# Weight sums of five product sets: made beside their use from quadrants loaded twice, instead of stored to and loaded from DRAM

## The chip, the core and the metric

The kernel runs on one core of a Trainium2 chip, all in float32. The metric is the device time of one execution in microseconds (us). TensorE multiplies, VectorE (DVE), ScalarE (ACT) and GpSimd (POOL) do elementwise work, and SyncE (SP) issues nearly all DMAs, in program order: a DMA whose data is not ready holds back every DMA behind it.

## What is computed

With x of 2048 rows by 512 columns (2 x 1024 x 512, flattened):

```python
xn = layernorm(x)
w_masked = weight * (block_sums(mask) > 0)      # 512 x 512, blocks of 32 x 32
s = xn @ w_masked.T
nx = xn * rsqrt(mean(xn**2) + 1e-5) * ln_w
g, u = nx @ gate_w.T, nx @ up_w.T               # 1792 wide each
ffn = (silu(g) * u) @ down_w.T
out = x + s * silu(ffn)
```

What matters here is `ln_w`, by which the columns of `gate_w` and `up_w` are scaled, and the mask on `weight`.

## The kernel before

**The algorithm.** Each matrix product is made by a seven-product scheme (of Strassen's kind, in Winograd's form) at two levels. At the outer level both matrices are cut in four quadrants. Seven "sets", numbered in the order 1, 2, 6, 5, 7, 3, 4, each multiply one weight block by one block of x. Sets 1 and 2 use weight quadrants as they are; sets 6, 5, 7, 3 and 4 use sums of quadrants (4 is a quadrant itself). Within a set the same scheme runs again with seven products of a 128 x 128 weight block by a 128 x 512 block of x, numbered 1, 5, 2, 6, 3, 7, 4 in their order in time.

**The groups.** The gate and up weights make seven groups (`G = 7`, g = 0 to 6), and the masked weight is an eighth (g = 7, `g == G` in the code). A group has four weight quadrants `(R, K)`, each 128 partitions by 512 columns (256 KB). `K` is the half of the columns that `ln_w` scales. Outer sums for one group are 7 = (0,0) - (1,0), 5 = (1,0) + (1,1), 6 = block 5 - (0,0) and 3 = (0,1) - block 6.

**The order of the work.** It is written out by hand. `at(pos, fn)` puts a call at a position; all calls are sorted by position and issued in that order (last lines of the kernel function). One position is one product of 512 columns, two matmul instructions. An *instance* is one set of one group, and starts every 7 positions. Part one runs sets 1 and 2 of all eight groups (instances 0 to 15, positions 0 to 111). Part two runs sets 6, 5, 7, 3, 4 of group 0, then of group 1 and so on (instances 16 to 55, positions 112 to 391). So a group in part two takes 35 positions; `rest` is the position of its first product. A third part multiplies by `down_w` in the same way (position 392 = `END` on).

**Inside an instance** (`instance`): at offsets 0, 2, 3, 4, 6, 8, 12 the products are made into PSUM banks X, Y and Z. Product 7 of an instance is added into the bank that product 6 has just filled, so a *snap*, a DVE add at offset 5 that reads the bank first, must be done by offset 8. A *seed*, an ACT copy at offset 1, fills bank Z before offset 3. The kernel divides PSUM into 8 banks of 512 columns: 3 of X, 2 of Y, 1 of Z and 2 of V; gates (`silu`) and a few others take turns in V.

**The weights before.** In part one, each group's four quadrants are loaded (`load_a`), scaled in SBUF on ACT (`scale_a`, two instructions of 256 columns per quadrant; for g = 7 `mask_a` on POOL), and POOL makes the four outer sums (`outer_a`, 128 x 512 each, at p + 1 where p is the position of the group's set 1; p + 15 for g = 7). `store_w` writes the five blocks (1280 KB) to `w_dram`. For part two `load_w` brings them back 29 positions ahead of the group (11 for g = 0). Four POOL instructions of 128 x 640 (`inner_a`, from rest - 13, or rest - 9 for g = 0) then make the inner sums of all five sets at once.

**What else the steps touch.** `summed` adds two finished results of a set on POOL or DVE, and `done` then makes silu(gate) x up for the set's rows: ACT's gate, DVE's multiplication (`h_out`, line 404), and `h_sum`, eight POOL subtractions per group, each stored to `h_dram` by SP. `outer_d(f)` makes the outer sums of the down weights of group f: four DVE operations of 128 x 256 at offsets 30 to 36 of the group's part two, and a store at 37. Almost every add stands under line 98, the helper `add`. The last set of the third part makes its last four products in two column halves (`last_four`), so that the end of the kernel (silu, multiply, add, store: `finish`) works on 256 columns.

Of the kernel before, what the change touches and what calls it, by code (L numbers as in the profile page):

```python
# [31 lines left out]
def tile_masked_linear_gated_ffn(  # L32
# [23 lines left out]
    dw_dram = tc.dram_tile([4, P, G, 256], F32, name="dw_dram")  # L56
    w_dram = tc.dram_tile([G + 1, P, 5, W], F32, name="w_dram")

# [30 lines left out]
    def slots(i, n):  # L89
        return mem[:, i : i + n, :]  # L90
# [3 lines left out]
    def bank(tag, name):  # L94
        return ps.tile([P, W], F32, tag=tag, name=name, bufs=PSB[tag])

    def add(eng, o, a, b, op=ALU.add):
        eng.tensor_tensor(o, a, b, op)  # L98
# [144 lines left out]
    BLOCKS = (6, 5, 7, 3, 4)  # L243
    aq, aop, ablk, wblk = {}, {}, {}, {}

    def q_slot(g):
        return F["v5"] + 4 if g % 2 else F["q"]

    def w_slots(g):

        if g == 0:
            return F["q"], F["a1"] + 4
        return (F["s"], F["s"] + 5) if g % 2 else (F["q"], F["a1"] + 4)

    def load_a(g, R, K):
        i = q_slot(g) + (1, 4)[K] if R else F["a1"] + 2 * (g % 3) + K
        aq[g, R, K] = mem[:, i, :]
        nc.sync.dma_start(aq[g, R, K], gu[g, R, K] if g < G else wm[R, K])

    def scale_a(g, R, K, eng=act):  # L260
        for c in range(2):
            v = aq[g, R, K][:, c * 256 : (c + 1) * 256]
            if eng is pool:
                nc.gpsimd.tensor_scalar(v, v, lnw_sb[:, 2 * K + c : 2 * K + c + 1], None, ALU.mult)
                continue
            nc.scalar.mul(v, v, lnw_sb[:, 2 * K + c : 2 * K + c + 1])

# [15 lines left out]

    def mask_a(R, K):
        v = aq[G, R, K].rearrange("p (b j) -> p b j", j=BLK)
        k = keep[:, 2 * R + K, :].unsqueeze(2).to_broadcast([P, 16, BLK])
        nc.gpsimd.tensor_tensor(v, v, k, ALU.mult)

    def outer_a(g, q, eng):

        o = ablk[g, q] = mem[:, q_slot(g) + BLOCKS.index(q), :]
        a, b, op = {
            7: lambda: (aq[g, 0, 0], aq[g, 1, 0], ALU.subtract),
            5: lambda: (aq[g, 1, 0], aq[g, 1, 1], ALU.add),
            6: lambda: (ablk[g, 5], aq[g, 0, 0], ALU.subtract),
            3: lambda: (aq[g, 0, 1], ablk[g, 6], ALU.subtract),
        }[q]()
        add(eng, o, a, b, op)

    def store_w(g):  # L300
        nc.sync.dma_start(w_dram[g], slots(q_slot(g), 5))

    def load_w(g):
        i, _ = w_slots(g)
        nc.sync.dma_start(slots(i, 5), w_dram[g])

# [81 lines left out]
    def group(g, where):  # L388
# [39 lines left out]
        def summed(dst, src, into, then=None, engines=(pool,) * 4):  # L428

            def after(i, pos):  # L430
                at(pos + 1.2, lambda: add(engines[i], into(i), dst(i), src(i)))
                if then:
                    then(i, pos + 3.2)
            return after
# [6 lines left out]
            5: (None, v5, summed(v5, acc, vc)),  # L441
            7: (acc, acc, summed(v5, acc, v5, done(1, 1, v5), (dve, dve, pool, pool))),
            3: (vc, vc, done(0, 1, vc)),
# [42 lines left out]
    def outer_d(f):  # L486

        a = slots(F["a1"] + 2, 2).rearrange("p s w -> p (s w)").rearrange("p (b w) -> p b w", w=256)
        o = mem[:, F["v5"] + 8, :].rearrange("p (b w) -> p b w", w=256)
        (a11, a12, a21, a22), (s3, s1) = (a[:, b] for b in range(4)), (o[:, b] for b in range(2))  # L490

        def load():
            for b in range(4):
                nc.sync.dma_start(a[:, b], down[b // 2, b % 2, :, f])

        def store():
            nc.sync.dma_start(dw_dram[0:2, :, f].rearrange("b p w -> p b w"), a[:, 0:2])
            nc.sync.dma_start(dw_dram[2:4, :, f].rearrange("b p w -> p b w"), o)

        return [load, lambda: add(dve, s3, a11, a21, ALU.subtract), lambda: add(dve, s1, a21, a22),  # L500
                lambda: add(dve, a11, s1, a11, ALU.subtract), lambda: add(dve, a12, a12, a11, ALU.subtract), store]

# [49 lines left out]
    def down_instance(o, q, where_, prior, dest, after):  # L552
# [7 lines left out]

        last_set, halves = q == DOWN[-1], (slice(0, W // 2), slice(W // 2, W))

        def last_four(products):

            four = [(lambda k=k: ds[q][4][:, k, :], lambda k=k: dt[q, 4][:, k, :]) for k in range(K3)]
            four.append((lambda: dq[q][:, G - 1, P :], lambda: dh[q][:, 0, G - 1, :]))
            for half in halves:
                for w, b in four:
                    def one(w=w, b=b, half=half):
                        nc.tensor.matmul(st[half.start][:, half], w(), b()[:, half], start=False, stop=True,  # L570
                                         skip_group_check=True)
                    products.append(one)

        def base_of_last():
            for half in halves:
                st[half.start] = bank("X", f"half_{half.start}")
                add(dve, st[half.start][:, half], st["x"][:, half], prior(2)[:, half])

        products = []
        for m, key in ((1, "x"), (5, "y"), (6, "x"), (2, "z"), (None, "z"), (None, "v"), (7, "x"), (3, "y"), (None, "y"),  # L580
# [9 lines left out]
            for k in range(K3):  # L590
                b = {1: lambda k=k: dh[q][:, 0, k, :], 2: lambda k=k: dh[q][:, 0, K3 + k, :],
                     3: lambda k=k: dh[q][:, 1, K3 + k, :]}.get(m, lambda k=k, m=m: dt[q, m][:, k, :])
                products.append((key, lambda k=k, m=m: ds[q][m][:, k, :], b, k == 0 and m in (1, 5)))
        assert len(products) == (29 if last_set else 25)
        for k, p in enumerate(products):
            if callable(p):
                at(where_(21) + (k - 21) / 2, p)
            else:
                at(where_(k), mm, k, *p)
# [29 lines left out]
        if last_set:  # L629
            at(where_(17) + 0.1, base_of_last)  # L630
            for half, pos in zip(halves, (where_(23), where_(25))):
                finish(1, 0, 2, yacc(2), pos, dve, half, lambda half=half: st[half.start][:, half])

# [14 lines left out]
    for K in range(2):  # L648
        at(T(-10), load_a, 0, 0, K)
    at(T(-10), load_x, 1)  # L650
    for R, K, g in ((0, 0, 1), (0, 1, 1), (1, 0, 0), (1, 1, 0)):
        at(T(-10), load_a, g, R, K)
    at(T(-10), load_x, 2)
    for R, K, g in ((0, 0, 2), (0, 1, 2), (1, 0, 1), (1, 1, 1)):
        at(T(-10), load_a, g, R, K)
    at(T(-10), load_x, 3)
# [13 lines left out]
    for i in range(TT):  # L670
# [5 lines left out]
        for c in range(KC):  # L676
            at(T((10.2, 10.6, 11.0, 11.8)[c] + 0.1 * i), transpose, 0, c, (2, 3, 0, 1)[i], "XYYX"[c])
            at(T(15.3 + 0.4 * c + 0.1 * i), transpose, 1, c, (2, 3, 0, 1)[i], "XVVY"[c])
    at(T(6.0), scale_a, 0, 0, 0, pool)
    at(T(8.2), scale_a, 0, 0, 1, pool)  # L680
    for c in range(KC):
# [5 lines left out]
    for q in (1, 2):  # L687
        for k in (0, 1):
            for n in (0, 1):
                at(8, outer_b, q, k, n, None)  # L690
    at(T(16.4), scale_a, 1, 0, 0)
    for pos, (R, K, g) in zip((5.2, 8.7, 9.8), ((0, 1, 1), (1, 0, 0), (1, 1, 0))):
        at(pos, scale_a, g, R, K)
    for i in range(TT):
# [26 lines left out]


    for g in range(G + 1):
        p, rest = 7 * where[g, 1], 7 * where[g, BLOCKS[0]]
        prepare = scale_a if g < G else lambda g, R, K: mask_a(R, K)
        for K in range(2):
            if g > 2:
                at(p - 22, load_a, g, 0, K)
            if g > 1:
                at(p - (10.4, 7.3)[K], prepare, g, 0, K)  # L730
                at(p - 10, load_a, g, 1, K)
            if g > 0:
                at(p - ((3.1, 1.9) if g != 2 else (4.3, 3.1))[K], prepare, g, 1, K)
        if g:
            plan(p - 7, 1, inner_a(g, 1))
        else:
            plan(T(7.4), 0, inner_a(0, 1, 0, 1))
            plan(T(10.0), 0, inner_a(0, 1, 1, 1))
        sums = {0: 10, G: p + 15}.get(g, p + 1)
        for i, q in enumerate((7, 5, 6, 3)):  # L740
            at(sums + 1.6 * i, outer_a, g, q, pool)
        at(sums + 7.5, store_w, g)
        at(rest - 29 if g else rest - 11, load_w, g)
        plan(rest - 13 if g else rest - 9, 2.5, inner_a(g, 2, 0, 5))
    for f in range(G):
        for off, fn in zip((8, 30, 32, 34, 36, 37), outer_d(f)):
            at(7 * where[f, BLOCKS[0]] + off, fn)
# [24 lines left out]
    for o, q in enumerate(DOWN):  # L772
        if o == 0:
            todo = [(p, 7 * where[4, 6] + 4 * k) for k, p in enumerate((b11, b12, b22, b21, e0, e1))]
        elif o == 1:
            todo = [(p, END - 22 + 7 * p[0]) for p in (b11, b21, e0, b12, b22, e1)]
        else:
            d = D(o - 2)
            todo = [(b11, d(4)), (b12, d(4) + 0.1), (b21, d(14)), (b22, d(21)), (e0, d(25) + 1), (e1, d(25) + 1.1)]
        for part, pos in todo:  # L780
            at(pos, load_h, q, (H0, H1)[o % 2], part)
# [94 lines left out]
```

## Time and profile before

| | |
|---|---|
| median of 3 runs (lowest, highest) | 524.22 us (522.89, 524.28) |
| the profiled execution's own time | 523.43 us |
| its span, first to last instruction | 521.6 us |
| granted TensorE clock | 0.999 |
| busy: PE, DVE, ACT, POOL | 508.3, 384.6, 153.4, 376.1 us |
| DMA | 138.35 MB, mean 265 GB/s |

The profiled execution's own time is 1.83 us more than its span. Times inside the trace are from the span's start. Part one runs to about 119.6 us, part two to about 365 us. In a timeline line the columns are start, length from the first start to the last end, engine, source line, operation, output<-input, shapes and a count; a bracket holds the idle time of the engine just before and what ended it. Matmuls of 512 columns start every 0.43 us when nothing holds them, though each is shown 0.59 us long, because they overlap: a pair is shown as 1.02 and takes 0.86, two pairs are shown as 1.88 and take 1.72. So a shown idle time of PE is some 0.16 us shorter than the time lost, which is best read from the distance between starts.

### The profile page before, as it was taken

What the parts mean: (1) busy time and instruction counts of PE and PEld (TensorE: products, weight loads), DVE (VectorE), ACT (ScalarE), POOL (GpSimd) and SP (SyncE); (2) the same over time, 40 slices, a digit from 0 to 9 for tenths busy, and PEclk for the clock granted to TensorE, in tenths of its full rate; (3) what the DMA queues carried; (4) which work ended last, traced back from release to release, by engine and by line L of the source; (5) the groups of instructions that cost most, each with busy time, mean ns of one, the idle gap of its engine ahead of it and who ended that gap; (6) DMA issues with size and microseconds to landing.
All of it is one profiled execution on the core that took longest, in us unless ns stands there. A gap on an engine that the chain in (4) does not pass through costs nothing.

```text
span 521.6 us, 4847 instructions
## 1 busy us (share of the span) xinstructions
PE 508.3 (97%) x1269; PEld 230.2 (44%) x1269; DVE 384.6 (74%) x557; ACT 153.4 (29%) x286; POOL 376.1 (72%) x301
## 2 busy tenths in 40 slices
PE   8999999989999999999999999998999999999996
PEld 8444543433444444444444444443444444444443
DVE  6898789846796968869696886989645655456735
ACT  3859764431232332223233222320101101001111
POOL 5596569987996978869688886967553564739960
PEclk9999999999999999999999999999999999999999
DMA  8579979779738485675988666599897599476472
GB/s 306 219 273 340 360 238 352 291 269 385 273 139 286 182 300 203 233 261 167 403 326 268 256 239 235 197 343 357 301 386 259 187 350 354 157 251 196 156 232 80
DMA packets 60314, 138.35 MB, mean 265 GB/s; under 512 B 5744, under 2 KB 13184, under 8 KB 56192
## 3 DMA queue, kind: packets, MB, share of 16 engines
q1 hardware_dynamic: 60000, 137.53, 73.4%
q10 hardware_dynamic: 288, 0.52, 0.3%
q8 instruction: 10, 0.16, 0.1%
q14 instruction: 16, 0.13, 0.1%
HBM read 81.40 MB, written 56.63 MB: 265 GB/s over the span
## 4 chain that ended last, share of the span: by engine, by line
PE 73%; DVE 11%; DMA 7%; POOL 4%; issue 3%; ACT 1%; SPq 0%; DVEq 0%; POOLq 0%
PE x L338 24%; PE dx L559 14%; PE y L338 13%; PE dy L559 8%; DVE mem L98 7%; PE z L338 6%; PE dz L559 5%; POOL mem L98 3%; DMA w_dram<-mem 2%; DVE mem L404 2%; DMA mem<-w_dram 2%; DMA mem<-h_dram 1%; PE dv L559 1%; DMA mem<-in_mask 1%; PE pt L156 1%
## 5 line engine op out<-in xcount | busy, mean ns | idle before, releaser
L98 POOL TENSOR_TENSOR mem<-mem 128x512 f32<-128x512 f32 (+4 forms) x266 | 343.3, 1311 | 108.8 <-ACT mem L363 24.5
L338 PE MATMUL x<-mem 128*128 128x512 f32 x448 | 214.5, 595 | 2.8 <-DVE mem L98 2.4
L338 PEld LDWEIGHTS x<-mem 128*128 128x128 f32 x448 | 83.3, 190 | 110.9 <-issue 90.4
L98 DVE TENSOR_TENSOR mem<-x,mem 128x512 f32<-128x512 f32 x136 | 92.3, 684 | 42.8 <-PE x L338 41.6
L338 PE MATMUL y<-mem 128*128 128x512 f32 x224 | 114.7, 594 | 3.1 <-POOL mem L98 1.9
L98 DVE TENSOR_TENSOR mem<-mem 128x512 f32<-128x512 f32 (+2 forms) x93 | 108.6, 1171 | 8.2 <-PE dx L559 4.4
L559 PE MATMUL dx<-mem 128*128 128x512 f32 x174 | 78.3, 592 | 0.0
L98 DVE TENSOR_TENSOR mem<-y,mem 128x512 f32<-128x512 f32 x96 | 65.7, 684 | 15.0 <-PE y L338 11.4
L338 PEld LDWEIGHTS y<-mem 128*128 128x128 f32 x224 | 41.9, 190 | 55.9 <-issue 45.6
L345 ACT COPY z<-x 128x512 f32<-128x512 f32 x55 | 31.4, 571 | 119.5 <-PE x L338 117.9
L338 PE MATMUL z<-mem 128*128 128x512 f32 x112 | 57.4, 594 | 0.8 <-ACT z L345 0.8
L559 PEld LDWEIGHTS dx<-mem 128*128 128x128 f32 x174 | 33.1, 190 | 41.6 <-issue 40.9
L559 PE MATMUL dy<-mem 128*128 128x512 f32 x98 | 44.5, 592 | 0.0
L399 ACT ACTIVATE gate<-mem 128x512 f32<-128x512 f32 x56 | 33.2, 603 | 21.5 <-DVE mem L98 11.2
L404 DVE TENSOR_TENSOR mem<-gate,mem 128x512 f32<-128x512 f32 x56 | 37.3, 678 | 0.5 <-ACT gate L399 0.3
L532 POOL TENSOR_TENSOR mem<-mem 128x512 f32<-128x512 f32 x16 | 24.4, 1526 | 17.7 <-DMA mem<-s_dram 17.4
L338 PEld LDWEIGHTS z<-mem 128*128 128x128 f32 x112 | 21.0, 190 | 27.3 <-issue 22.7
L98 DVE TENSOR_TENSOR mem<-z,mem 128x512 f32<-128x512 f32 x41 | 28.0, 682 | 4.6 <-PE z L338 3.2
L559 PEld LDWEIGHTS dy<-mem 128*128 128x128 f32 x98 | 18.6, 190 | 23.4 <-issue 23.0
L542 ACT ACTIVATE silu<-mem 128x512 f32<-128x512 f32 x15 | 9.0, 602 | 64.6 <-DVE mem L98 48.3
L98 DVE TENSOR_TENSOR mem<-dx,mem 128x512 f32<-128x512 f32 x16 | 11.1, 691 | 20.0 <-PE dx L559 20.0
L559 PE MATMUL dz<-mem 128*128 128x512 f32 x56 | 25.2, 592 | 0.0
(61 smaller groups left out, 222.9 us busy)
## 6 DMA issues: line engine op xcount, KB each, us to landing
h_dram<-mem SPq DMA_DIRECT2D x98, 256.0 KB, 2.6
mem<-h_dram SPq DMA_DIRECT2D x28, 768.0 KB, 6.5
w_dram<-mem SPq DMA_DIRECT2D x8, 1280.0 KB, 6.1
mem<-w_dram SPq DMA_DIRECT2D x8, 1280.0 KB, 8.2
acc_dram<-mem SPq DMA_DIRECT2D x8, 1024.0 KB, 6.3
mem<-acc_dram SPq DMA_DIRECT2D x8, 1024.0 KB, 4.8
mem<-in_gu SPq DMA_DIRECT2D x28, 256.0 KB, 5.0
s_dram<-mem SPq DMA_DIRECT2D x16, 256.0 KB, 4.5
```

What stands on the lines that cost most here:

```text
L98: eng.tensor_tensor(o, a, b, op)
L156: nc.tensor.transpose(pt[t, c][:, i * P : (i + 1) * P], xt[t, i][:, c * P : (c + 1) * P], ident)
L338: nc.tensor.matmul(st[key], weights(g, q, m), operand(q, m), start=first and not (key == "z" and seeded), stop=True, skip_group_check=True)
L345: nc.scalar.copy(st["z"], st["x"])
L399: nc.scalar.activation(gate[key], t(), AF.Silu)
L404: nc.vector.tensor_mul(a(), gate[key], b())
L532: at_later.append(lambda: nc.gpsimd.tensor_tensor(s_tile, s_tile, rms_bc[t], ALU.mult))
L542: nc.scalar.activation(b[0][:, part], y[:, part] if source is None else source(), AF.Silu)
L559: nc.tensor.matmul(st[key], w(), b(), start=first and key != "z", stop=True, skip_group_check=True)
```

## The change

- `store_w`, `load_w`, `w_dram` and the sums of part one are gone. Part one loads, scales and uses only the two quadrants with R = 0.
- In part two, `load_block` loads all four quadrants of a group 29 positions ahead, by four DMAs of 256 KB. `outer_a` returns nine steps, at rest - 19.9 to rest - 13.95: ACT makes two scaled blocks in SBUF (four instructions of 256 columns) and three scaled copies in banks of V (six instructions of 256 columns), and DVE makes four sums of 512 columns that each read one such bank. Group 7 has its four quadrants masked on POOL at rest - 20.5, and ACT's copies are plain ones of 512 columns.
- `inner_a` of part two starts at rest - 13 for every group.
- `outer_d`: ACT copies two blocks into a V bank, three DVE sums read the bank, the fourth sum goes to POOL; offsets 24.6 to 27.5, and the store at 30.
- Set 7 of group 7 makes all four `summed` adds on POOL; two of them were on DVE.
- The last four products are made in three column parts of 256, 128 and 128.

```diff
-    def store_w(g):
-        nc.sync.dma_start(w_dram[g], slots(q_slot(g), 5))
-    def load_w(g):
-        nc.sync.dma_start(slots(i, 5), w_dram[g])
+    def scaled(o, a, g, K, eng=act):
+        if g == G:
+            if o is not a:
+                nc.scalar.copy(o, a)
+            return
+        for c in range(2):
+            cols, w = slice(c * 256, (c + 1) * 256), lnw_sb[:, 2 * K + c : 2 * K + c + 1]
+            if eng is pool:
+                nc.gpsimd.tensor_scalar(o[:, cols], a[:, cols], w, None, ALU.mult)
+            else:
+                nc.scalar.mul(o[:, cols], a[:, cols], w)
+    def load_block(g):
+        i, _ = w_slots(g)
+        wblk[g] = [mem[:, i + k, :] for k in range(5)]
+        for k, (R, K) in ((1, (1, 0)), (4, (1, 1)), (0, (0, 0)), (3, (0, 1))):
+            nc.sync.dma_start(wblk[g][k], gu[g, R, K] if g < G else wm[R, K])
+    def outer_a(g):
+        b = wblk[g]
+        v = {}
+        def in_bank(k, K):
+            v[k] = bank("V", f"a{k}_{g}")
+            scaled(v[k], b[k], g, K)
+        return [lambda: scaled(b[2], b[1], g, 0), lambda: scaled(b[4], b[4], g, 1), lambda: in_bank(1, 0),
+                lambda: in_bank(0, 0), lambda: add(dve, b[1], v[1], b[4]),
+                lambda: add(dve, b[2], v[0], b[2], ALU.subtract), lambda: add(dve, b[0], b[1], v[0], ALU.subtract),
+                lambda: in_bank(3, 1), lambda: add(dve, b[3], v[3], b[0], ALU.subtract)]
...
-            7: (acc, acc, summed(v5, acc, v5, done(1, 1, v5), (dve, dve, pool, pool))),
+            7: (acc, acc, summed(v5, acc, v5, done(1, 1, v5), (dve, dve, pool, pool) if g < G else (pool,) * 4)),
...
-        return [load, lambda: add(dve, s3, a11, a21, ALU.subtract), lambda: add(dve, s1, a21, a22),
-                lambda: add(dve, a11, s1, a11, ALU.subtract), lambda: add(dve, a12, a12, a11, ALU.subtract), store]
+            v[0] = bank("V", f"down_{f}").rearrange("p (b w) -> p b w", w=256)
+            nc.scalar.copy(v[0], a[:, 0::2])
+        return [load, in_bank, lambda: add(dve, s3, v[0][:, 0], a21, ALU.subtract), lambda: add(dve, s1, v[0][:, 1], a22),
+                lambda: add(dve, a11, s1, v[0][:, 0], ALU.subtract), lambda: add(pool, a12, a12, a11, ALU.subtract), store]
...
-        last_set, halves = q == DOWN[-1], (slice(0, W // 2), slice(W // 2, W))
+        last_set, parts = q == DOWN[-1], (slice(0, W // 2), slice(W // 2, 3 * W // 4), slice(3 * W // 4, W))
...
-        sums = {0: 10, G: p + 15}.get(g, p + 1)
-        for i, q in enumerate((7, 5, 6, 3)):
-            at(sums + 1.6 * i, outer_a, g, q, pool)
-        at(sums + 7.5, store_w, g)
-        at(rest - 29 if g else rest - 11, load_w, g)
-        plan(rest - 13 if g else rest - 9, 2.5, inner_a(g, 2, 0, 5))
+        at(rest - 29, load_block, g)
...
+        at(rest - 20, block_sums)
+        if g == G:
+            for k, (R, K) in ((1, (1, 0)), (4, (1, 1)), (0, (0, 0)), (3, (0, 1))):
+                at(rest - 20.5, lambda k=k, R=R, K=K: mask_a(wblk[G][k], R, K))
+        for k, off in enumerate((-19.9, -19.3, -18.1, -17, -15.95, -15.94, -15.93, -15.3, -13.95)):
+            at(rest + off, lambda g=g, k=k: todo[g, k]())
+        plan(rest - 13, 2.5, inner_a(g, 2, 0, 5))
     for f in range(G):
-        for off, fn in zip((8, 30, 32, 34, 36, 37), outer_d(f)):
+        for off, fn in zip((8, 24.6, 26.05, 26.06, 26.07, 27.5, 30), outer_d(f)):
             at(7 * where[f, BLOCKS[0]] + off, fn)
```

## The prediction, made before the changed kernel had run

> **What bounds the kernel.** I read the busy times by stage first, then what PE waits for, then the places of those waits in the timeline. Columns of the stages: stretch, its length, busy time (and count) of PE, PE's weight loads, DVE, ACT, POOL, then clock and DMA.
>
> ```profile
> 15.00:120.00 105.00, 100.34 (x265) 45.02 (x266) 85.09 (x142) 63.63 (x130) 78.13 (x74) 1.00 0.79 293
> 151.00:334.00 183.00, 181.69 (x421) 79.14 (x419) 147.22 (x229) 51.38 (x91) 148.56 (x110) 1.00 0.72 254
> 334.00:366.00 32.00, 30.49 (x70) 13.24 (x71) 29.79 (x38) 6.14 (x11) 22.98 (x16) 1.00 0.89 323
> 366.00:514.00 148.00, 148.00 (x346) 65.54 (x345) 84.42 (x85) 17.02 (x29) 87.17 (x60) 1.00 0.71 251
> ```
>
> PE is the bound nearly everywhere. The change leaves its products as they are, so only PE's holes, the start and the tail can move. The waits of PE (total us, times, longest) name who makes the holes:
>
> ```profile
> PE x L338 <- DVE mem L98: 2.4, 9, 0.4
> PE y L338 <- POOL mem L98: 1.9, 1, 1.9
> PE y L338 <- DVE mem L98: 1.2, 1, 1.2
> PE z L338 <- ACT z L345: 0.8, 2, 0.5
> PE pm L281 <- DVE mem L404: 0.6, 1, 0.6
> PE x L338 <- DMA mem<-w_dram: 0.3, 1, 0.3
> ```
>
> Three kinds of place, from the timelines of PE, DVE, POOL and ACT:
>
> ```profile
> 104.98 1.88 PE L338 MATMUL x<-mem 128*128 128x512 f32 x4
> 108.73 1.12 PE L338 MATMUL y<-mem 128*128 128x512 f32 x2 [1.86 <-POOL mem L98]
> ...
> 241.68 1.02 PE L338 MATMUL x<-mem 128*128 128x512 f32 x2
> 242.93 1.13 PE L338 MATMUL x<-mem 128*128 128x512 f32 x2 [0.23 <-DVE mem L98]
> ...
> 361.33 1.88 PE L338 MATMUL x<-mem 128*128 128x512 f32 x4
> 364.37 1.13 PE L338 MATMUL y<-mem 128*128 128x512 f32 x2 [1.16 <-DVE mem L98]
> ```
>
> At 108.73 two pairs should have taken 1.72; the distance is 3.75, so 2.03 are lost, and 0.10 more because the pair after a stall takes 0.96 (1.12 shown) and not 0.86. In this way I get all holes after 30 us:
>
> - Part one: 0.56 (40.20, snap late on DVE), 0.53 (42.45, seed late on ACT), 0.37 (80.7, DVE), 0.73 (85.80, DVE), 2.13 (108.73, POOL), and 0.77 at 119.61 and 123.24 (the load from `w_dram`, then POOL's 640-wide sums behind it). Sum 5.09.
> - At the group borders of part two, a hole of 0.49 at 154.77, 181.86, 212.39, 242.93, 303.50 and 334.02. Sum 2.94.
> - Before the third part 0.60 (352.64) and 1.42 (364.37). Sum 2.02.
>
> **Part one.** Removed from POOL: 32 outer sums at 1.27 each, 41 us, of which ten lie in this one stretch:
>
> ```profile
> 81.48 21.80 POOL L98 TENSOR_TENSOR mem<-mem 128x512 f32<-128x512 f32 x17
> ```
>
> POOL ran without a gap up to the late inner sum at 107.95 that PE waits for. Ten sums and two maskings less there are 14.8 us; the hole of 2.13 goes, and nothing else is near: DVE sat idle 4.1 us before 112.47. The 0.77 goes too: group 0's quadrants are now loaded some 25 us ahead (29 positions of 0.8585), and POOL's inner sums move from 119.70 into an idle time that it had there (4.3 us, waiting for `w_dram`) and into what is freed. 42.45: ACT did the R = 1 scalings (0.41 apart) and waited 0.59 for one of group 2's or 3's quadrants just before the table load and the gates that delayed the seed. With 28 ACT instructions less in part one it is early: 0.53 goes. 40.20: DVE worked without a gap from 28.2 to 40 and three tiny operations took 0.64, 0.52 and 1.02 where the same ones elsewhere take 0.31, 0.16 and 0.16; POOL's outer sums ran all that time. They are gone, DVE gains some 1.5, and 0.56 goes. 80.7 and 85.80: here DVE was held in an add of 1.74 beside POOL's sums of x, which stay. I take half of 1.10. Part one: 2.13 + 0.77 + 0.53 + 0.56 + 0.55 = **-4.5**; bounds -5.1 and -2.9 (only the first two).
>
> **The group border in part two.** Before, DVE is held by one SBUF sum of `outer_d` and the snap comes late:
>
> ```profile
> 239.05 1.28 DVE L404 TENSOR_TENSOR mem<-gate,mem 128x512 f32<-128x512 f32 x2
> 240.25 1.43 DVE L98 TENSOR_TENSOR mem<-mem 128x256 f32<-128x256 f32 x1
> 241.60 0.68 DVE L98 TENSOR_TENSOR mem<-z,mem 128x512 f32<-128x512 f32 x1
> 242.20 0.68 DVE L98 TENSOR_TENSOR mem<-x,mem 128x512 f32<-128x512 f32 x1
> ```
>
> The same sum takes 0.41 when POOL does not run beside it, and DVE operations that read a PSUM bank take 0.68 whether it runs or not. So this 1.43 is gone. What is late next? I followed both queues by hand through this group (its first product at 241.68).
>
> DVE: a queued add takes 0.60. The snap at 228.14 is followed by three of the new sums (to 230.55), set 7's first `summed` add, a total, the fourth new sum (231.75 to 232.35) and the second `summed` add. The total that was made at 231.65 starts at 233.1 and ends at 233.8; the product that needs it is due at 241.68 - 9 x 0.8585 = 233.95. Just in time. ACT's copies are no limit: loads issued near 219.7, 5.0 to landing (median of `in_gu`), seed to 225.3, four scalings of 0.41 to 227.0, and bank copies of 0.37 to 0.50 per 256 columns (a silu of 256 columns between banks, a scaling within SBUF; no row has this pairing): the second copy is there by 228.5, needed at 229.35.
>
> POOL: its first 640-wide sum now reads the fourth new sum and starts at 232.45, not 230.90. From there to the end of set 7's third `summed` add it needed 238.66 - 230.90 = 7.76; now a 256-wide down sum (0.73) stands before that add, and 0.18 of a collision with DVE goes. It ends at 240.75. DVE's second gate multiplication reads it, and that stood at 239.65: DVE waits, and behind it in the queue are z's total and the snap, which ends at 242.63. PE wants it at 242.54 (242.93 before). **So the new wait takes the place of most of the old one**: 0.24 instead of 0.49, six times: **-1.5**. Bounds: 0 (-2.9), and 0.25 worse each (+1.5), since every 0.1 that POOL starts later is 0.1 for PE.
>
> [...]
>
> **Before the third part.** DVE sheds two adds (0.88 and 1.04) between 352.5 and 355, but POOL's `h_sum`s, 0.75 later by the above, hold SP's load of the first down quadrant (issued at 340.58, 6.3 to landing), for which POOL waited 4.29 at 346.92 and, behind it, DVE and PE at 352.64. From there PE, not DVE, sets the times until the last 1536-wide adds. I take **+0.5**; bounds -1.4 (two adds less) and +1.2.
>
> **Tail.** The last columns go through silu, multiply and add at 128 instead of 256 columns (0.37, 0.42, 0.42), but DVE has two operations more in a queue that is full from 516.2. **-0.2**; bounds -0.4 and +0.8 (16 matmuls of 128 columns at 0.11 like the transposes, or at the 0.19 of a weight load). DMA moves 16 x 1280 KB less and 16 x 256 KB more, 16.8 of 138 MB; in the stage where it was fullest no wait of PE is on a transfer that this makes shorter, so I count 0.
>
> **Sum.** -4.5 - 1.5 + 0.5 - 0.2 = -5.7. Against the profiled execution's 523.43 this is **517.7 us**. The three runs' median is 0.8 above that execution, the lowest 0.5 below.
>
> **Rivals.**
> 1. *The border stays.* POOL's late start eats all of the group's gain, or up to 0.25 more each. For: the snap misses by 0.1 as it is. Against: POOL has 5.8 idle of 30.5 per group. Time: 523.43 - 4.5 + 0.5 - 0.2 = 519.2, up to 520.7.
> 2. *All holes of part two go* (POOL starts early enough), and all of part one's: 523.43 - 5.1 - 2.9 - 1.0 = 514.4.
> 3. *A loop of transfers and sums bounds the group: slower.* SP issues the loads behind the sixth `h_sum` store of the group before. From that sum's end: 0.45 to issue, 5.0 landing, ACT to the second bank copy 3.15, DVE's queue to the fourth sum 3.1, POOL from the first 640-wide sum to the next sixth `h_sum` 17.9 (230.90 to 249.05 before, less 0.74 idle and 0.25 of collisions, plus the 0.73): 29.6, against 35 x 0.8585 = 30.05 for PE. It decides from 0.45 us more. At the 6.9 of `in_down` in place of 5.0 it is 31.5, 1.45 per group, six groups: 523.43 - 4.5 + 8.7 = 527.6. For: before, this loop was some 3 us shorter, as POOL read the loaded blocks directly. Against: fewer bytes are under way, and 5.0 was measured in the fuller part one.
> 4. *It does nothing*: part one's waits reappear on DVE, the border stays: 522 to 525.
>
> **Numbers.** Chances: forecast 0.48, rival 1 0.16, rival 2 0.09, rival 3 0.20, rival 4 0.07. What this kernel's measurement can tell from no change is about 0.3%, 1.6 us. Forecast, rival 2 and most of rival 1 are faster by more: 0.72. Rival 4 and the rest of 1: 0.08. Rival 3: 0.20. The range runs from rival 2 to just short of rival 3's middle, for its mild end is likelier than 6.9: 514.4 to 525.5.
>
> **What would show it.** Right: no wait of PE on POOL at 108 or on a load at 119; part two begins some 4 us earlier against its first product; at each border DVE's gate multiplication waits for POOL for about 1 us, and PE's hole is 0.1 to 0.4; no DVE sum of 256 columns over 0.5. Wrong: groups longer than 30.5 with ACT waiting for `in_gu` in part two (rival 3), a hole at 9 positions ahead of each border (DVE's queue), or seeds late on ACT.

## The result, and the profile after

The changed kernel takes **520.47 us** (median of 4 runs, 520.12 to 521.38) against 524.25 of the kernel before in the same session (4 runs, 522.89 to 524.47): ratio **0.9936, 95% interval 0.9914 to 0.9958**. It is faster, by 3.8 us where 5.7 were forecast. The profiled execution has 520.12, its span is 518.3, the granted clock 1.0.

The stages of the changed kernel, in the columns used for before (stretch, its length, busy time and count of PE, weight loads, DVE, ACT, POOL, clock, DMA); the limits are moved by what PE had gained:

```profile
15.00:116.40 101.40, 99.00 (x265) 45.22 (x266) 85.76 (x145) 57.10 (x112) 47.91 (x49) 1.00 0.49 178
147.30:330.40 183.10, 182.69 (x422) 79.41 (x422) 148.88 (x248) 78.12 (x151) 152.71 (x119) 1.00 0.69 245
330.40:363.00 32.60, 30.11 (x70) 12.94 (x69) 27.60 (x34) 5.85 (x11) 28.88 (x20) 1.00 0.83 302
363.00:511.00 148.00, 148.00 (x346) 65.49 (x346) 85.21 (x86) 17.02 (x29) 87.79 (x60) 1.00 0.73 252
```

Part one has lost 30 us of POOL's work. In part two ACT now works 78 us instead of 51 (the scalings of the quadrants loaded again, and the copies into PSUM), POOL 4 more. The stretch before the third part has grown, and POOL with it, from 23 to 29. What PE waits for:

```profile
PE x L343 <- DVE mem L97: 1.7, 4, 1.0
PE y L343 <- DVE mem L97: 1.5, 1, 1.5
PE idle L678 <- POOL ident masks.py:199: 1.4, 1, 1.4
PE pm L304 <- DVE mem L409: 0.8, 1, 0.8
```

PE's wait for POOL at 108 and that for `w_dram` are gone; the one at `ident` lies in the start of the kernel, and the profile before has it too. (Of the small holes at the borders this view shows only a part; I read all holes from the distances of PE's products.) The three places that the prediction quoted, in PE's timeline:

```profile
104.28 1.88 PE L343 MATMUL x<-mem 128*128 128x512 f32 x4
106.00 1.02 PE L343 MATMUL y<-mem 128*128 128x512 f32 x2
...
237.29 2.13 PE L343 MATMUL x<-mem 128*128 128x512 f32 x4
...
358.07 1.88 PE L343 MATMUL x<-mem 128*128 128x512 f32 x4
361.42 1.12 PE L343 MATMUL y<-mem 128*128 128x512 f32 x2 [1.47 <-DVE mem L97]
```

At 106.00 the product that waited 1.86 for POOL follows its forerunner at once. At the border four matmuls are shown as 2.13 where 1.88 is normal: a hole of 0.25, forecast 0.24. The four matmuls at 358.07 start 3.35 before the next, at 361.42: 1.63 lost, and 0.10 in the pair behind; before, 1.42 in all. And DVE at that border, in time order:

```profile
235.06 0.68 DVE L409 TENSOR_TENSOR mem<-gate,mem 128x512 f32<-128x512 f32 x1
236.36 0.69 DVE L409 TENSOR_TENSOR mem<-gate,mem 128x512 f32<-128x512 f32 x1 [0.62 <-POOL mem L97]
236.97 0.68 DVE L97 TENSOR_TENSOR mem<-z,mem 128x512 f32<-128x512 f32 x1
237.56 1.28 DVE L97 TENSOR_TENSOR mem<-x,mem 128x512 f32<-128x512 f32 x2
```

The add of 1.43 is gone from the queue; the second gate multiplication waits 0.62 for POOL, and the snap that PE needs stands right behind it.

**Where the time went.** PE does the same products in the same order up to the last columns, so I compare the starts of the same PE instruction (number 100, 380, 860, 940 and the end). Number 380 stands 14 positions into part two, so that the first stretch holds the waits at its beginning too; number 940 is the first of the third part. "Before again" is a second profile of the kernel before, taken as the last experiment.

| stretch, us | before | before again | after | change | forecast |
|---|---|---|---|---|---|
| start to number 100 | 18.14 | 18.68 | 18.55 | +0.41 / -0.13 | 0 |
| part one, to 380 | 116.07 | 116.40 | 112.02 | -4.05 / -4.38 | -4.5 |
| part two, to 860 | 208.93 | 208.86 | 208.62 | -0.31 / -0.24 | -1.5 |
| before the third part, to 940 | 36.35 | 36.19 | 37.36 | +1.01 / +1.17 | +0.5 |
| third part and tail | 142.08 | 142.1 | 141.76 | -0.3 | -0.2 |
| span | 521.6 | 522.2 | 518.3 | -3.3 / -3.9 | -5.7 |

So part one brought what was forecast; part two brought almost nothing, and the end took back more. The experiments are mostly about these two.

### The profile page after: what moved, and what is told of

It is laid out like the page before. It is cut to its first block, busy times and chain, and to the rows that moved or that the text cites. A ratio compares the mean times of both kernels' runs of the same rounds, so it can differ in the third digit from the quotient of the medians.

```text
span 518.3 us, 4933 instructions
## 1 busy us (share of the span) xinstructions
PE 507.8 (98%) x1277; PEld 231.2 (45%) x1277; DVE 384.5 (74%) x583; ACT 177.8 (34%) x340; POOL 341.8 (66%) x280
## 5 line engine op out<-in xcount | busy, mean ns | idle before, releaser
L97 POOL TENSOR_TENSOR mem<-mem 128x512 f32<-128x512 f32 (+4 forms) x243 | 306.4, 1285 | 139.1 <-ACT mem L264 45.6
L97 DVE TENSOR_TENSOR mem<-mem 128x512 f32<-128x512 f32 (+2 forms) x64 | 83.8, 1315 | 7.7 <-PE dx L570 4.2
```

## The experiments

All start from the changed kernel. Their times are single executions, if not said otherwise, beside 523.8 to 525.1 of the kernel before; what is read is mostly the length of a stretch in the profile, which repeats within 0.1 us where no transfer decides. All of them together, the stretches as above:

| run | part one | part two | before third | rest | us |
|---|---|---|---|---|---|
| after | 112.02 | 208.62 | 37.36 | 141.76 | 520.12 |
| 1 down sum later | 112.02 | 207.70 | 38.04 | 141.76 | 519.90 |
| 2 loads of h later | 112.03 | 208.08 | 37.52 | 141.77 | 519.79 |
| 3 first down quadrant earlier | 112.02 | 209.65 | 36.17 | 141.77 | 519.98 |
| 4 mask product later | 111.02 | 208.50 | 37.28 | 141.76 | 519.19 |
| 5 DVE sums back (attention set) | 112.03 | 210.02 | 36.92 | 141.76 | 521.16 |
| 6 down sums from SBUF, old places | 112.02 | 218.03 | 36.88 | 141.78 | 529.37 |
| 7 POOL sums back in part one | 117.52 | 209.07 | 37.94 | 141.76 | 526.69 |
| 8 second loads later | 112.02 | 227.67 | 37.42 | 141.76 | 539.66 |
| 9 three undone | 112.02 | 222.45 | 36.13 | 142.71 | 533.86 |
| four edits (1 to 4) | 111.03 | 206.19 | 36.50 | 141.77 | 516.08 |
| five edits | 111.02 | 206.20 | 34.51 | 141.76 | 513.83 |

**1. What holds the border.**

```
-    for off, fn in zip((8, 24.6, 26.05, 26.06, 26.07, 27.5, 30), outer_d(f)):
+    for off, fn in zip((8, 24.6, 26.05, 26.06, 26.07, 28.5, 30), outer_d(f)):
```

> POOL's 256-wide down sum stands behind set 7's last sum on POOL, not ahead of it. My theory (the border's hole of 0.24 is DVE's second gate multiplication waiting 0.62 us for POOL, and POOL is late by the 0.74 us of the down sum): the gate multiplication waits no more, the six borders' holes of 0.23 to 0.25 fall to 0.05 or less, part two gets shorter by 1.0 to 1.5 us; the holes at 260.12 (0.36) and 349.39 stay. Rival (DVE's own queue is full there, the gate multiplication being only where the wait shows): the wait goes, the holes stay at 0.2 or more. Second rival (POOL's late first 640-wide sum alone): holes fall to 0.1 to 0.2.

DVE at the same border:

```profile
234.39 1.30 DVE L409 TENSOR_TENSOR mem<-gate,mem 128x512 f32<-128x512 f32 x2
235.60 0.68 DVE L97 TENSOR_TENSOR mem<-z,mem 128x512 f32<-128x512 f32 x1
236.20 1.28 DVE L97 TENSOR_TENSOR mem<-x,mem 128x512 f32<-128x512 f32 x2
```

The two gate multiplications follow each other without a wait, and no hole is left at any border. My theory holds for the border: one 256-wide sum of 0.74 on POOL, put one place too early, is worth 0.24 each. But part two is only 0.92 shorter and the kernel gains only 0.2: the holes that were expected to stay grew, in group 5 by 0.7 and before the third part by 0.7. PE runs 0.9 ahead there, and what it waits for comes hardly earlier: group 5's first quadrant lands at 252.46 instead of 252.24, the first down quadrant at 343.33 instead of 343.54.

**2. Group 5.**

```
-            parts = [(p, 7 * where[4, 6] + 4 * k) for k, p in enumerate((b11, b12, b22, b21, e0, e1))]
+            parts = [(p, 7 * where[4, 6] + 8 + 4 * k) for k, p in enumerate((b11, b12, b22, b21, e0, e1))]
```

> The six 512 to 768 KB loads of h for the first down set are issued eight positions later in group 4, so that SP issues the quadrants of group 5 ahead of them. My theory (group 5's quadrants are late because SP issues them behind two of these loads, and share the transfers with them): ACT's wait of 1.02 us for in_gu at 252.27 goes, the hole at 260.12 (0.36) goes and the one at 269.13 (0.44) falls to the 0.24 of the other borders: 0.4 to 0.6 us in all. Rival (SP is held by POOL's late stores of h sums, whatever the loads): the issue stays at 246.1 or later against PE's products, and both holes stay.

ACT in group 5, first in the changed kernel, then in the experiment:

```profile
252.27 1.71 ACT L264 ACTIVATE mem<-mem,lnw_sb 128x256 f32<-128x256 f32 x4 [1.02 <-DMA mem<-in_gu]
```

```profile
251.20 1.70 ACT L264 ACTIVATE mem<-mem,lnw_sb 128x256 f32<-128x256 f32 x4
```

The wait for the load is gone, and with it the hole at 260.12 and the excess at 269.13: -0.55, as expected. The rival is right on one point: SP issues the quadrants only 0.22 earlier (245.94 instead of 246.16), since a store of an h sum stands before them in both. What changed is the way to landing, a median of 3.5 us instead of 6.3, with two loads of h of 768 KB less issued in the six microseconds ahead of them. In the changed kernel and runs 1, 3, 4 and 5, which keep the early loads of h, ACT's wait here was 1.02, 2.16, 2.03, 0.94 and 2.38, and part two between 207.7 and 210.0 (run 1, with no border holes, the lowest). This one place depends on the luck of the transfers, by up to 1.4 us; neither profile of the kernel before has a wait on a load here.

**3. The end of part two.**

```
-        at((END - 29.8, END - 14, END + 7)[o] if o < 3 else D(o - 2)(4), load_d, q, QD[o % 3])
+        at((END - 34.9, END - 14, END + 7)[o] if o < 3 else D(o - 2)(4), load_d, q, QD[o % 3])
```

> The load of the first down quadrant (896 KB) is issued five positions earlier, ahead of four of the late stores of h sums in SP's queue. My theory (this load, held by those stores, sets when POOL's sums for the third part run, and so the holes at 349.39, 1.28 us, and 361.42, 1.73 us): it is issued 2.5 to 4 us earlier, POOL's idle time of 2.46 at 343.67 goes, the hole at 349.39 falls below 0.5 and the two together by 1.0 to 2.0. Rival (the 1536-wide adds on DVE, 2.2 to 2.6 us each beside POOL's sums, set it): POOL runs earlier, the hole at 361.42 stays within 0.3 and the sum of the two falls by less than 0.6.

POOL before the third part, changed kernel and experiment:

```profile
343.67 18.22 POOL L97 TENSOR_TENSOR mem<-mem 128x384 f32<-128x384 f32 x12 [2.46 <-DMA mem<-in_down]
```

```profile
329.08 29.81 POOL L97 TENSOR_TENSOR mem<-mem 128x640 f32<-128x640 f32 x21
```

SP issues the load at 333.52 instead of 337.68, POOL no longer waits, and the two holes of 1.28 and 1.73 become 0.94 and 0.89: 1.2 us. (The first was expected below 0.5.) Here PE came 1.0 late out of group 5, which flatters this; in the run with four edits, where PE came early, the stretch still takes 36.50 instead of the 38.04 of run 1. And counted from PE's number 860, SP issued this load 2.56 us ahead in both profiles of the kernel before, but only 1.51 ahead in the changed one: 1.05 later, as much as the end lost. So POOL's late h sums, which hold SP, are most of it. The rival has a part too: DVE's add of 128x1536 at 358.88 took 1.74, with POOL done by then, against 2.57 at 358.19 in the changed kernel.

**4. The hole at 85.10.**

```
-    at(76, mask_blocks)
+    at(80, mask_blocks)
```

> PE's 64-column product of the mask sums and the small DVE operation behind it stand four positions later. My theory (the hole of about 0.9 at 85.10, which the change made 0.18 longer, is PE waiting for a V bank that a late gate multiplication on DVE still reads, and nothing behind it is late): the hole falls to 0.3 or less and everything behind it is 0.5 to 0.9 us earlier up to 147. Rival (DVE is late for the next snap or total anyway, held by its adds of 1.74 and 1.37 beside POOL's): PE waits as long at one of the next four products, and nothing is gained by 95.

PE around it, changed kernel and experiment:

```profile
82.27 2.07 PE L343 MATMUL x<-mem 128*128 128x512 f32 x4
85.10 0.41 PE L304 MATMUL pm<-mask_sums,blockones 128*128 128x64 f32 x2 [0.76 <-DVE mem L409]
```

```profile
85.27 1.88 PE L343 MATMUL x<-mem 128*128 128x512 f32 x4
86.98 1.02 PE L343 MATMUL y<-mem 128*128 128x512 f32 x2
87.84 0.33 PE L304 MATMUL pm<-mask_sums,blockones 128*128 128x64 f32 x2
```

The small product goes through without a wait, nothing else comes late, and part one is 1.00 shorter; it is kept to the end. The products behind did not need DVE to be earlier: only the mask product, which waits for a bank, did.

**5. One part undone: the sums of the attention set.**

```
-            7: (..., (dve, dve, pool, pool) if g < G else (pool,) * 4)),
+            7: (..., (dve, dve, pool, pool))),
```

> One part undone: in the attention set (the last group of part two) two of set 7's 512-wide sums go back from POOL to DVE. My theory (in DVE's queue near 350 to 361 two sums more, of 0.7 to 1.0 us beside POOL, cost more than POOL's late end): the hole at 361.42 (1.73) grows by 0.3 to 1.5, that at 349.39 stays within 0.3. Rival (POOL's two extra sums keep it busy beside DVE's 1536-wide adds and slow these down, 2.2 to 2.6 us each instead of 1.75): the adds get shorter and the two holes together fall by 0.3 or more.

The hole at 361 did not grow: 1.41 instead of 1.73, that before it 1.17 instead of 1.28. The stretch is 0.44 shorter, and DVE's third 1536-wide add took 2.02 instead of 2.41. My theory falls; the rival's direction is right. But PE came 1.5 late out of group 5 in this execution, so how much of the 0.44 belongs to the edit is open.

**6. One part undone: the down weights' sums as before.** The sums read SBUF, without the copy into PSUM, the fourth is on DVE again, at the old places:

```
-        v[0] = bank("V", f"down_{f}").rearrange("p (b w) -> p b w", w=256)
-        nc.scalar.copy(v[0], a[:, 0::2])
+        v[0] = a[:, 0::2]
...
-    for off, fn in zip((8, 24.6, 26.05, 26.06, 26.07, 27.5, 30), outer_d(f)):
+    for off, fn in zip((8, 24.6, 30, 32, 34, 36, 37), outer_d(f)):
```

> One part undone: the four 256-wide sums of the down weights are made on DVE from SBUF, 30 to 36 positions into the group as before the change, and the copy into PSUM is gone. My theory (POOL's late start makes DVE wait, and an add of 1.43 us that DVE makes beside POOL comes on top): an SBUF sum of 1.0 to 1.5 us stands in DVE's queue next to each border again, and the borders' holes are 0.5 to 0.9 instead of 0.24, part two 1.5 to 4 us longer. Rival (the wait for POOL and the add lie beside each other, as POOL no longer has the 0.74 us sum): the holes are as before the change, 0.45 to 0.5, part two 1.2 to 1.6 us longer.

DVE at the first border:

```profile
145.10 0.69 DVE L409 TENSOR_TENSOR mem<-gate,mem 128x512 f32<-128x512 f32 x1 [0.48 <-POOL mem L97]
145.71 1.14 DVE L97 TENSOR_TENSOR mem<-mem 128x256 f32<-128x256 f32 x1
146.77 0.68 DVE L97 TENSOR_TENSOR mem<-z,mem 128x512 f32<-128x512 f32 x1
147.37 0.68 DVE L97 TENSOR_TENSOR mem<-x,mem 128x512 f32<-128x512 f32 x1
147.97 1.51 DVE L97 TENSOR_TENSOR mem<-mem 128x256 f32<-128x256 f32 x1
```

The wait for POOL and an add of 1.14 stand one behind the other, and a second add of 1.51 follows. Each makes its own hole, of 0.78 and 0.73 (at 148.10 and 152.27 here), so that an ordinary group takes 1.26 more than in the changed kernel: part two is 9.4 longer, the whole 8.9. Both expectations were too small, and neither had the second hole. Without this part of the change the other parts would have made the kernel slower than before: 529.4 against 524.0.

**7. POOL's load in part one put back.**

```
+    def extra(g, k):
+        if g < G:
+            o = mem[:, (F["v5"] + 4 if g % 2 else F["q"]) + k, :]
+            add(pool, o, aq[g, 0, 0], aq[g, 0, 1])
...
+        for k in range(4):
+            at({0: 10, G: p + 15}.get(g, p + 1) + 1.6 * k, extra, g, k)
```

> Work added that nobody reads: four 512-wide sums on POOL per set of weights in part one (28 in all, 1.27 us each), at the positions where the outer sums stood before the change. My theory (POOL's queue alone made the hole of 2.13 us at 108.73, and its sums beside DVE those of 0.56 and 0.37 near 40 and 81): the hole at 108 comes back with 1.0 to 2.2, at 80 to 86 0.2 to 0.6 more are lost, in all +1.5 to +3.5 by 130. Rival (the stored weights and their loads, ACT's scalings and SP's queue made them): less than 0.5 comes back.

What the expectation did not see: the extra sums of group 6 write where group 0's second quadrants have just been loaded, so this run computes with other weights there, and ACT waits for those sums. PE and POOL near the old hole:

```profile
106.39 1.88 PE L343 MATMUL x<-mem 128*128 128x512 f32 x4
109.86 1.12 PE L343 MATMUL y<-mem 128*128 128x512 f32 x2 [1.59 <-POOL mem L97]
112.29 1.13 PE L343 MATMUL z<-mem 128*128 128x512 f32 x2 [1.31 <-ACT z L350]
```

```profile
82.89 21.64 POOL L97 TENSOR_TENSOR mem<-mem 128x512 f32<-128x512 f32 x17
```

POOL has the 17 gapless sums of the kernel before again (21.80 us there), and PE's wait for POOL is back: 1.75 lost at 109.86, and 0.10 behind it, where the kernel before lost 2.13. Near 40, holes of 0.55, 0.36 and 0.83 (each with 0.1 behind it) are there, 2.0 in all against 1.1 in the kernel before: two small operations of DVE (lines 171 and 138) took 0.70 and 0.93 and a 512-wide one (line 146) 1.60, against 0.16, 0.16 and 0.54 in the changed kernel. That is my theory, with 3.9 of the 5.5 us, more than its 1.5 to 3.5. The 1.58 at 112.29 come from the overlap and tell nothing. At 81 nothing came back.

**8. The price of the loop.**

```
-        at(rest - 29, load_block, g)
+        at(rest - 26.8, load_block, g)
```

> The quadrants that are loaded a second time are issued 2.2 positions (1.9 us) later. It prices the slower case of my prediction (loads, ACT, DVE, POOL, stores, loads bound the group). In an ordinary group the first issue is at 155.02, some 4.5 us to landing, the first scaling at 160.30: 0.8 us of slack. My theory (a loop, with little to spare): the second copies into PSUM come 1.0 to 1.5 us late, a hole of 0.7 to 1.4 appears nine positions ahead of each border, and the whole is 4 to 8 us longer, slower than before the change. Rival (the slack of ACT, DVE and POOL takes it up): less than 1.5 us in all.

PE's waits in this run, the two largest, and PE behind the longest one:

```profile
PE z L343 <- ACT z L350: 10.7, 6, 6.0
PE x L343 <- DVE mem L97: 5.2, 9, 1.7
```

```profile
270.76 2.07 PE L343 MATMUL z<-mem 128*128 128x512 f32 x2 [5.99 <-ACT z L350]
272.62 3.62 PE L343 MATMUL x<-mem 128*128 128x512 f32 x4
```

And ACT in the first group of part two:

```profile
162.54 0.91 ACT L264 ACTIVATE mem<-mem,lnw_sb 128x256 f32<-128x256 f32 x2 [1.76 <-DMA mem<-in_gu]
```

19.5 us slower, not 4 to 8. First, 2.2 positions put the loads behind the stores of an h sum and of a gate product and four loads of down weights in SP's queue: they are issued at 159.12 instead of 155.02, 4.1 us later and not 1.9. Second, the scalings that wait hold everything behind them on ACT, the next set's seed too: PE then waits for the seed (6.0 at the worst, in group 5). The first group that suffers loses 2.0, the next 1.6 and 2.4, group 5 8.4, the last two together 4.4. Some 2.6 of the 8.4 are not waiting: behind the wait of 5.99, the pair starts 1.86 ahead of the next product, where pairs behind shorter waits take 0.96, and four matmuls are shown as 3.62 that are shown as 1.88 elsewhere. The granted clock of this run is 0.992 in the mean, against 1.0 in the changed kernel.

**9. Three things undone, each in a stretch of its own**: the loads at the start put back; the down sums from SBUF, but at the new places; the last columns in halves.

```
+    for K in range(2):
+        at(T(-10), load_r, 0, K)
...
-        v[0] = bank("V", f"down_{f}").rearrange("p (b w) -> p b w", w=256)
-        nc.scalar.copy(v[0], a[:, 0::2])
+        v[0] = a[:, 0::2]
...
-        last_set, parts = q == DOWN[-1], (slice(0, W // 2), slice(W // 2, 3 * W // 4), slice(3 * W // 4, W))
+        last_set, parts = q == DOWN[-1], (slice(0, W // 2), slice(W // 2, W))
```

> Three things undone, each in a stretch of its own. (1) Start: the four loads of 256 KB that stood between the loads of x are issued again, to memory that nobody reads. If their absence made PE 0.41 us late by 18 us, the product at 18.55 is back at 18.1 to 18.2; rival (luck of the transfers and of DVE beside POOL): it stays at 18.5 to 18.9. (2) Part two: the three sums of the down weights on DVE read SBUF, at the places where they stand now (24.6 to 26 positions), without the copy into PSUM. If the PSUM source matters, each takes 0.9 to 1.5 us instead of 0.41, and holes of 0.5 or more come at or ahead of each border, part two 3 to 10 us longer; rival (only the place in the queue mattered in the run with the old places, which took 8.9 us more): less than 1.5 us longer. (3) Tail: halves of 256 columns instead of the last 256 in two parts: the end is 0.2 to 0.4 later against its products; rival: no difference over 0.1.

Start: the product is at 18.78; the rival's luck, not the loads. Part two: 13.8 longer, more than the 3 to 10 expected and worse than at the old places, so the source matters more than the place. DVE's three sums, first in the changed kernel, where each has one of its two inputs in the copy's bank, then here, with both in SBUF:

```profile
200.66 0.74 DVE L97 TENSOR_TENSOR mem<-down,mem 128x256 f32<-128x256 f32 x2
201.44 0.42 DVE L97 TENSOR_TENSOR mem<-mem,down 128x256 f32<-128x256 f32 x1
```

```profile
205.02 3.95 DVE L97 TENSOR_TENSOR mem<-mem 128x256 f32<-128x256 f32 x3
```

1.2 us against 3.95. POOL's four 640-wide sums beside them run from 202.24 to 208.69, and DVE's three end at 208.97, 0.28 behind; a group later POOL ends at 241.02 and DVE at 241.31. The kernel before shows the same: of its 30 sums of 256 columns from two SBUF inputs, the 15 that began while a POOL sum had 0.3 us or more to go ended 0.28 behind that sum and took 0.60 to 1.52; the other 15 took 0.41 to 0.42. In the changed kernel, 21 of the 256-wide sums with one input in a bank began while a POOL sum ran, and took 0.41 to 0.42.

Tail: from the first product of the last columns to the end of the last add 4.94 us, as in the kernel before (4.94), against 4.80 in the changed kernel: 0.14 of the forecast 0.2. The rest of this run's 0.95 lies behind the last add, in the last transfer and the end of the program, and is not explained.

**The four edits together.**

> Together: the down sum behind set 7's last sum on POOL, the loads of h eight positions later, the first down quadrant five positions earlier, the mask product four positions later. If the four causes are independent places: -1.2 to -1.5 (six borders), -0.55 (group 5), -1.0 (85), and at the end the holes of 1.28 and 1.73 fall to 0.8 each or less (-1.0 to -1.4): 515.5 to 516.8 us. Rival (POOL's own time, 30.05 us less little per group, is the limit once PE's holes go): part two is no more than 1.0 shorter, and holes of over 0.3 appear nine positions ahead of the borders or at 349; 517.5 or more.

516.08 us. In sum the places add up: part two is down to 206.2, against 206.1 for 480 matmuls at 0.4293. The first theory holds: POOL is no limit yet. The end did not come as expected: of its two holes the first is gone, and the second is left with 1.92, at 357.28. DVE's queue suggests why, an add of 128x1536 ahead of the snap of bank y:

```profile
354.04 2.58 DVE L97 TENSOR_TENSOR mem<-mem 128x1536 f32<-128x1536 f32 x1
356.55 0.68 DVE L97 TENSOR_TENSOR mem<-y,mem 128x512 f32<-128x512 f32 x1
```

**Five edits**, with that add moved:

```
-            pos = END + (-26, -17, -8, -5)[k] if o == 0 else D(o - 1)((3, 8, 12, 18)[k])
+            pos = END + (-26, -17, -8, 9)[k] if o == 0 else D(o - 1)((3, 8, 12, 18)[k])
```

> The four edits of the run before, and DVE's fourth 1536-wide add, of 2.58 us, fourteen positions later, behind set 4's totals, where DVE then stands idle for 3.8 us. My theory (the hole left at 357.28, 1.92 us, is a snap of bank y held in DVE's queue behind this add, which nobody needs before 20 products of the third part): the hole falls below 0.4, 514.0 to 514.6 us. Rival (the snap is late for the add at 350.24 too, or the third part's next products wait for the moved add): 0.8 or more of the 1.92 stays or comes back by 376; 515.0 or more.

All that the view of PE's waits lists for this kernel:

```profile
PE idle L678 <- POOL ident masks.py:199: 1.4, 1, 1.4
PE z L343 <- ACT z L350: 0.5, 1, 0.5
PE x L343 <- DVE mem L97: 0.4, 1, 0.4
```

**513.83 us** (5 runs, 513.45 to 513.92) against 524.78 (9 runs): ratio **0.9795, interval 0.9781 to 0.9808**. The hole is gone and nothing comes back, so that add was its cause. What is left lies in the first 29 us, but for some 0.2 each at 83, 318 and 345.

**The kernel before once more.**

> The kernel before the change once more, unchanged, for a second profile of it. In nine profiles of the changed kernel and its variants the product that stood at 18.14 in the profile before starts at 18.55 to 18.92; the loads put back did not bring it back. If the change makes the start late, it is at 18.1 to 18.3 here; if it is luck of that one profile, at 18.5 to 18.9, and then 0.4 of the comparison of the two profiles is no effect of the change. Its holes at 40, 42, 81, 86, 108, 119 and 123 (5.1 in all), six of 0.49 at the borders and two before the third part (2.0) should all be within 0.1 of the first profile; where one differs by more, that place depends on the luck of the transfers.

PE in part one of this second profile:

```profile
81.55 1.13 PE L338 MATMUL x<-mem 128*128 128x512 f32 x2 [0.47 <-DVE mem L98]
...
85.67 1.12 PE L338 MATMUL x<-mem 128*128 128x512 f32 x2 [0.42 <-DVE mem L98]
87.55 0.41 PE L281 MATMUL pm<-mask_sums,blockones 128*128 128x64 f32 x2 [0.76 <-DVE mem L404]
...
109.45 1.12 PE L338 MATMUL y<-mem 128*128 128x512 f32 x2 [0.83 <-POOL mem L98]
```

The start is at 18.68, so the 0.41 was luck of the first profile. The holes of part one are not fixed: 2.43 in three places at 80 to 88 (1.10 in two before) and 1.10 at 109 (2.13 before), together 3.53 and 3.23: with more lost at 80, less is lost at 109. The hole at 42.45, where PE waited for ACT's seed, is not there; one of 0.39 stands at 44.69 instead. The borders are the same 0.48, and before the third part 0.42 and 1.42 are lost (0.60 and 1.42 in the first profile).

## Why the prediction was right, and where its sizes failed

- **The whole: -3.8 of the forecast -5.7.** 520.47 lies where rival 1 (the border stays) put its time, 519.2 to 520.7, and not near the forecast's 517.7. Part one is the forecast's, and part two brought as little as in rival 1, but only partly for rival 1's reason: at the five borders where there was a hole before, POOL's late start left half of it (at the last 0.42 of 0.49), much as the forecast has it; the rest was lost at places that neither had.
- **Part one, -4.5: right in sum** (-4.05 and -4.38 against the two profiles). POOL's queue as the cause of the hole at 108, and of the slow small operations on DVE near 40, is shown by run 7; the end of the wait on `w_dram` is seen in the waits. That ACT's scalings made the 0.53 at 42.45 is not shown: the second profile of the kernel before has no wait for the seed there, and run 7 lost more near 40 without these scalings. One term failed, "I take half of 1.10" for the pair at 80.7 and 85.80: after, 1.2 is lost there, against 1.10 and 2.43 in the two profiles before. What is lost there varies from one execution to the next, so that it was no term to be halved; the hole at the mask product needed no faster DVE but another place for that product (run 4).
- **Borders, six times 0.49 to 0.24, -1.5: mechanism right, sum wrong.** The hole and its cause came as worked out (0.25; run 1), with a wait for POOL of 0.62 where about 1 was expected, and no down sum on DVE took over 0.42. I counted the holes of before and priced these places. One of the six I read wrongly: the hole at 154.77 is not at a border but four products behind one, and it is gone. But the new hole comes at every border, at 147.44 and 269.13 too, where before there was none of this kind (+0.24 each), the last one stayed 0.42, and one of 0.19 at 321.07 is new, its cause open. And in group 5 the slower rival came true, in one group of six: loads behind late h sums and 768 KB transfers, 0.55 (run 2), by luck up to 1.4 more in other executions. Measured: -0.3.
- **Rival 3, the loop**, was placed rightly: run 8, with loads 4.1 us later, went over its margin. How large the margin is (0.45 by the sum) was not measured. Its way to PE was another: the sum lets the lateness go on through DVE and POOL, but PE is first held by ACT's queue, where the seed stands behind the scalings (the prediction has late seeds only among its signs).
- **Before the third part, +0.5: mechanism right, size +1.0 to +1.2**, inside its bounds. Of "DVE sheds two adds" run 5 shows no gain, though PE's late arrival in that run leaves it open. SP's late load of the first down quadrant, run 3, was most of it.
- **Tail, -0.2**: -0.14 in the engines' queues, -0.3 by the ends.
- The forecast counts nothing for a bank as a source of DVE's sums, and the rows agree: 0.41 to 0.42 for the 256-wide sum with a bank (changed kernel) and 0.41 from SBUF (run 6, where POOL did not hold it up); 0.68 for both kinds at 512.
- What the prediction did not ask is what the down weights' part is worth on its own. It booked it as the 1.43 that goes. Run 6 gives 8.9 us: without this part, the other parts would have lost more in part two than they gain in part one.

## What to carry to other kernels

When work is moved into a stage, price the new hole at every repetition of the stage, not only at the places where the old hole was, and look for the one repetition with other traffic in it. Twice here a wait that runs through two engines' queues hung on a single short instruction: before giving an engine less work, look whether that instruction, a 0.74 us sum or a 64-column product, can stand one place later. And where two parts of a change are made together, ask what each costs without the other.

## What the runs showed of the hardware

- A VectorE sum of 256 columns from two SBUF inputs took 0.41 to 0.42 alone or when it began ahead of a GpSimd sum (kernel before, run 6), and 0.60 to 1.52 when a GpSimd sum was already running (kernel before; 1.14 and 1.51 in run 6; three in a row 3.95 in run 9); with one input in PSUM 0.41 to 0.42 beside GpSimd sums (changed kernel). At 128x1536, in the changed kernel: 1.75 alone or begun ahead of the GpSimd sum, up to 2.57 begun behind it.
- ScalarE's scaling of 256 columns took 0.49 to 0.52 within SBUF and 0.46 to 0.48 into PSUM (changed kernel).
- A load of 256 KB at one place in group 5 landed 3.5 us after its issue (median of four, run 2), or 6.3 to 7.4 with two loads of 768 KB issued just ahead of it.
- After TensorE had waited 5.99 us, its next pair of matmuls took 1.86 (0.96 behind shorter waits) and the four behind it were shown as 3.62 (1.88 elsewhere); the mean granted clock of that run was 0.992 (run 8).
